# A fused two-block transformer kernel: row sums of the local softmax moved behind the next slot's transposes, and a scheduling fence behind the gated product

## The chip, the cores and the metric

The kernel runs on one core of a Trainium2 chip, as one launch. A core has a matrix engine (PE), a vector engine (DVE), an activation engine (ACT), a general engine (POOL) and a queue engine (SP) that issues the transfers. Each works through its own list of instructions in the order in which they were written down at build time; between engines only semaphores order the work. The metric is the device time of the launch in microseconds (us): the median of three runs of the kernel before is 5724.81 us (5724.38 to 5730.4).

## What is computed

The input is `x`, 8 batches of 512 tokens of width 128, in float32. The first part adds a causal attention with 16 heads of width 8, whose weights come from four Newton steps and not from a softmax. The change does not touch it. The second part is a small transformer of 6 layers on the layer-normed result; in each layer, for each batch:

```
q, k, v = split(shift(x) @ Wqkv)                # 16 heads of width 64
q, k    = rotary(l2norm(q) * qs), rotary(l2norm(k) * ks)
attn    = softmax(8 * q @ k.T, over a window of 32 back)
x       = x + (attn @ v) @ Wo
a, gate = split(layernorm(shift(x)) @ W1 + b1)  # 341 columns each
x       = x + (a * gelu(gate)) @ W2 + b2
```

`shift` moves half of the channels by one token. A softmax row is exp(s - max) divided by its own sum: that sum and the division are the steps that the change moves. The "first factor" of the feed-forward is `a`, and its products with W1 are those called `ap` in the code.

## The kernel before

The second part treats a layer, a batch and half of the heads (8 of 16) as a *half*, and each half as four *pairs* of heads. One turn of the loop in lines 713 to 753 is a *slot*; eight slots are one batch of one layer, so there are 48 batches to go through. In slot t four pieces of work overlap:

- the pair of slot t is begun. `turn` (L528) transposes its queries and keys on PE into `ptq` and copies them by ACT into `qT` (L540). `weigh` (L543) multiplies them into the scores `s` (L559), lets DVE find the row maxima and subtract them (L565, L566, into the tile `pr`), ACT take the exponential (L570), DVE sum each row (L572, `rs`) and invert the sum (L573), and POOL multiply the row by it (L574);
- the pair of slot t-2 (`LAG` is 2) is ended. `turn_weights` (L578) transposes `pr` on PE into `pT` (L584) and copies it by ACT into `prT` (L585); `gather` (L587) multiplies by the values into `po` (L594), copied by ACT (L601); `leave` (L603) adds the output product into `acc` (L607);
- a quarter of the half after the next is prepared. `prepare_qk` multiplies for the queries and keys (`m`, L476); ACT squares (L481), DVE sums (L482) and applies the rotary tables (L484, L492), POOL adds and normalizes (L496, L504), with an inverse root in between (L499 on DVE, L500 and L501 on ACT). `prepare_v` makes the values (`pv`, L512) and ACT copies them (L516) into `v`; after the fourth quarter `spread` (L518) copies `v` by four transfers on SP into the layout `v3`. There is one `v` tile, so the next copy into it waits for these transfers;
- one step of the feed-forward of the batch before: a generator (L622) that is advanced once per slot at L741. Its steps are the shifted input, the mean, the variance, the products `gp` of the gate (L645) with DVE adding the bias (L648), the products `ap` of the first factor (L655) with DVE multiplying them into the gate (L658), and the last product `y` (L665). The gelu of the gate (L618) is put by `gelus` (L613) between two fences of one slot, because it needs another activation table.

Below, the slot whose feed-forward step makes `ap` is called the *ap slot*, and the next one the *y slot*. In program order the DVE multiplications L658 come at the end of the ap slot.

PSUM tiles with the tag "mm" (`ptq`, `pT`, `m`, `pv`, `gp`, `ap`, `y` and others) share four buffers, which go round. A product can be started only when the engine that reads the old contents of its buffer is done. `pr` has three buffers, `rs` two.

The order of the instructions on each engine isn't the order of the program text. A list scheduler goes over all instructions at build time, with its own estimates of when inputs are ready, and takes among ready ones the earliest in the text. A fence (`tc.no_sync_barrier()`) is a rule for that scheduler alone: on each engine, what stands in the text before the fence is put before what stands after it. It adds no instruction and no semaphore.

Of the kernel before, what the change touches and what calls it, by code (L numbers as in the profile page):

```python
# [49 lines left out]
def tile_kernel(  # L50
# [402 lines left out]
    def shifted(b, name):  # L453

        xs = tp.tile([P, N], F32, name=name)
        hf = D // 2
        nc.gpsimd.tensor_copy(xs[0:hf, :], xT[0:hf, b, :])
        nc.gpsimd.memset(xs[hf:D, 0:1], 0.0)
        nc.gpsimd.tensor_copy(xs[hf:D, 1:N], xT[hf:D, b, 0 : N - 1])
        return xs  # L460
# [67 lines left out]
    def turn(a):  # L528

        g, p = a["g"], a["p"]  # L530
        a["qT"] = qT = []
        for t in range(2):
            pt = ps_a.tile([P, N], F32, name="ptq", tag="mm")
            for c in range(NT):
                nc.tensor.transpose(  # L535
                    pt[:, c * P : (c + 1) * P],
                    g["qn"][t][:, c, 2 * p : 2 * p + 2, :].rearrange("p h e -> p (h e)"), ident,
                )
            q = tp.tile([P, N], F32, name=f"qT{t}")
            nc.scalar.copy(q, pt)  # L540
            qT.append(q)

    def weigh(a):  # L543

        qT = a["qT"]
        a["pr"] = pr = tp.tile([P, 2, NT, KB], F32, name="pr", bufs=3)
        nm = tp.tile([P, 2, NT], F32, name="nm")
        s = [ps_b.tile([P, NT, KB], F32, name="s2") for e in range(2)]
        for e in range(2):
            nc.tensor.matmul(  # L550
                s[e].rearrange("p c k -> p (c k)"), lhsT=ident_h,
                rhs=band.rearrange("p c k -> p (c k)"), start=True, stop=False,
            )
        for n in range(NQ):
            c, u = n // 2, n % 2
            k0 = max(n * QB - WIN, 0)
            for e in range(2):
                hr = slice(e * DHL, (e + 1) * DHL)
                nc.tensor.matmul(  # L559
                    s[e][u * QB : (u + 1) * QB, c, KB - (n + 1) * QB + k0 : KB],  # L560
                    lhsT=qT[0][hr, n * QB : (n + 1) * QB], rhs=qT[1][hr, k0 : (n + 1) * QB],
                    start=False, stop=(n >= NQ - 2),
                )
        for e in range(2):
            nc.vector.tensor_reduce(nm[:, e], s[e], axis=AX.X, op=ALU.max, negate=True)  # L565
            nc.vector.tensor_tensor(  # L566
                pr[:, e], s[e], nm[:, e].unsqueeze(2).to_broadcast([P, NT, KB]), ALU.add
            )
        flat = pr.rearrange("p e c k -> p (e c) k")
        nc.scalar.activation(flat, flat, AF.Exp)  # L570
        rs = tp.tile([P, 2 * NT], F32, name="rs")
        nc.vector.tensor_reduce(rs, flat, axis=AX.X, op=ALU.add)  # L572
        nc.vector.reciprocal(rs, rs)  # L573
        nc.gpsimd.tensor_tensor(  # L574
            flat, flat, rs.unsqueeze(2).to_broadcast([P, 2 * NT, KB]), ALU.mult
        )

    def turn_weights(a):  # L578
        pr = a["pr"]
        a["prT"] = prT = tp.tile([KB, 2, NT, P], F32, name="prT")  # L580
        for e in range(2):
            pT = ps_a.tile([KB, NT, P], F32, name="pT2", tag="mm")
            for c in range(NT):
                nc.tensor.transpose(pT[:, c, :], pr[:, e, c, :], ident)  # L584
            nc.scalar.copy(prT[:, e], pT)  # L585
# [36 lines left out]
    def feed_forward(b, l, w1, w2):  # L622

        xs = shifted(b, "xf")
        yield
        mean = ps_a.tile([P, N], F32, name="mean", tag="mm")
        nc.tensor.matmul(mean, lhsT=ones_d, rhs=xs, start=True, stop=True)
        nc.vector.tensor_tensor(xs, xs, mean, ALU.subtract)
        sq = tp.tile([P, N], F32, name="sq")
        nc.scalar.activation(sq, xs, AF.Square)  # L630
        yield
        var = ps_a.tile([P, N], F32, name="var", tag="mm")
        nc.tensor.matmul(var, lhsT=ones_d, rhs=sq, start=True, stop=True)
        rn = tp.tile([P, N], F32, name="qr")
        nc.scalar.activation(rn, var, AF.Ln, bias=eps_ln)
        nc.scalar.activation(rn, rn, AF.Exp, scale=-0.5)
        nc.gpsimd.tensor_tensor(xs, xs, rn, ALU.mult)
        xn = tp.tile([P, N], F32, name="xn_ffn", bufs=1)
        nc.gpsimd.tensor_scalar(
            xn, xs, vec[:, 0, l : l + 1], vec[:, 1, l : l + 1], ALU.mult, ALU.add  # L640
        )
        yield
        for k, (c0, cn) in enumerate(CH):
            gp = ps_a.tile([P, N], F32, name="gp", tag="mm")
            nc.tensor.matmul(  # L645
                gp[:cn], lhsT=w1[:, DI + c0 : DI + c0 + cn], rhs=xn, start=True, stop=True
            )
            nc.vector.tensor_scalar(  # L648
                gate[:cn, k], gp[:cn], vec[:cn, 3 + NCH + k, l : l + 1], None, ALU.add
            )  # L650
        waiting.append(gate)
        yield
        for k, (c0, cn) in enumerate(CH):
            ap = ps_a.tile([P, N], F32, name="ap", tag="mm")
            nc.tensor.matmul(  # L655
                ap[:cn], lhsT=w1[:, c0 : c0 + cn], rhs=xn, start=True, stop=True
            )
            nc.vector.scalar_tensor_tensor(  # L658
                gate[:cn, k], ap[:cn], vec[:cn, 3 + k, l : l + 1], gate[:cn, k],
                ALU.add, ALU.mult,  # L660
            )
        yield
        y = ps_a.tile([P, N], F32, name="y2", tag="mm")
        for k, (c0, cn) in enumerate(CH):
            nc.tensor.matmul(  # L665
                y, lhsT=w2[:cn, k, :], rhs=gate[:cn, k], start=(k == 0), stop=(k == NCH - 1)
            )
        nc.vector.scalar_tensor_tensor(
            xT[:, b, :], y, vec[:, 2, l : l + 1], xT[:, b, :], ALU.add, ALU.add
        )  # L670
        if l == DEPTH - 1:
            yield
            pf = ps_a.tile([P, NT, D], F32, name="pf", tag="mm")
            for c in range(NT):
                nc.tensor.transpose(pf[:, c, :], xT[:, b, c * P : (c + 1) * P], ident)
            nc.vector.tensor_tensor(x2[:, b], x2[:, b], pf, ALU.add)
            nc.sync.dma_start(out[b].rearrange("(c p) d -> p c d", p=P), x2[:, b])
# [13 lines left out]
    def open_half(i):  # L691
        l, b, hv = halves[i]
        groups.append(begin(l, b, hv, shifted(b, "xs") if hv == 0 else groups[-1]["xs"]))
# [17 lines left out]
    pairs, parts, acc = [], [], None  # L711
    t = -1
    while t < len(halves) * PH + LAG or parts:
        i, p = t // PH, t % PH
        a = done = ahead = None
        if 0 <= i < len(halves):
            a = dict(g=groups[i], p=p)
            pairs.append(a)
        if LAG <= t < len(pairs) + LAG:
            done = pairs[t - LAG]  # L720
        if a:
            turn(a)
        if done:
            turn_weights(done)

        i, c = (t + 1) // PH + 1, (t + 1) % PH
        if i < len(halves):
            if c == 0:
                open_half(i)
            ahead = groups[i]  # L730
            prepare_qk(ahead, wq[ahead["hv"]], tab[ahead["l"]], c)
        gelus()
        if a:
            weigh(a)
        if done:
            gather(done)
        if ahead:
            prepare_v(ahead, wq[ahead["hv"]], c)
            if c == PH - 1:
                prepared(ahead)  # L740
        parts = [n for n in parts if next(n, n) is not n]  # L741
        if done:
            l, b, hv = (done["g"][n] for n in ("l", "b", "hv"))
            if done["p"] == 0 and hv == 0:
                acc = ps_c.tile([P, N], F32, name="acc")
            leave(done, wo[hv], acc)
            if done["p"] == PH - 1:
                if b == NB - 1 and l + 1 < DEPTH:
                    wo[hv] = load_wo(l + 1, hv)
                if hv == 1:  # L750
                    nc.vector.tensor_tensor(xT[:, b, :], xT[:, b, :], acc, ALU.add)
                    parts.append(feed_forward(b, l, *w12[l]))
        t += 1
# [51 lines left out]
```

## Time and profile before

| quantity | value |
|---|---|
| median of three runs | 5724.81 us |
| the profiled execution, its own time | 5724.38 us |
| its span, first to last instruction | 5722.4 us |
| PE busy | 4686.3 us (82% of the span) |
| DVE busy | 4775.5 us (83%) |
| ACT busy | 4038.0 us (71%) |
| POOL busy | 3250.3 us (57%) |
| PE busy from 2600 to 3100 us | 484.67 of 500 us |
| DVE busy in the same stretch | 409.62 of 500 us |

The first part lasts until about 2100 us, and there DVE and ACT are the busiest. In the second part PE is busy nearly always, with its clock granted in full. The page's shares are means over both parts; a timeline lists the instructions of one engine in the order of time, with the idle time before each in brackets, and what ended it.

### The profile page before, as it was taken

What the parts mean: (1) busy time and instruction counts of PE and PEld (TensorE: products, weight loads), DVE (VectorE), ACT (ScalarE), POOL (GpSimd) and SP (SyncE); (2) the same over time, 40 slices, a digit from 0 to 9 for tenths busy, and PEclk for the clock granted to TensorE, in tenths of its full rate; (3) what the DMA queues carried; (4) which work ended last, traced back from release to release, by engine and by line L of the source; (5) the groups of instructions that cost most, each with busy time, mean ns of one, the idle gap of its engine ahead of it and who ended that gap; (6) DMA issues with size and microseconds to landing.
All of it is one profiled execution on the core that took longest, in us unless ns stands there. A gap on an engine that the chain in (4) does not pass through costs nothing.

```text
span 5722.4 us, 108133 instructions
## 1 busy us (share of the span) xinstructions
PE 4686.3 (82%) x40909; PEld 2744.5 (48%) x40909; DVE 4775.5 (83%) x12028; ACT 4038.0 (71%) x6458; POOL 3250.3 (57%) x2915
## 2 busy tenths in 40 slices
PE   4556566655666549999999999999999999999998
PEld 2223333332333225556656555555555655556665
DVE  8889898998989858888888888888888888888886
ACT  5788888888888856666666666666666666666665
POOL 1333233333323347777777677777777777777774
PEclk6555555555555569999999999999999999999999
DMA  0000000000000011111111211122111111121111
GB/s 17 1 0 1 1 1 1 1 1 0 1 1 1 1 39 44 44 47 47 46 44 42 58 47 40 39 51 53 44 44 44 52 44 42 47 58 45 47 42 34
DMA packets 106558, 173.16 MB, mean 30 GB/s; under 512 B 12816, under 2 KB 30008, under 8 KB 106040
## 3 DMA queue, kind: packets, MB, share of 16 engines
q1 hardware_dynamic: 106040, 166.25, 11.7%
q8 instruction: 325, 5.32, 0.4%
q14 instruction: 193, 1.58, 0.1%
HBM read 19.42 MB, written 2.10 MB: 4 GB/s over the span
## 4 chain that ended last, share of the span: by engine, by line
PE 39%; DVE 33%; ACT 20%; POOL 5%; issue 2%; DMA 0%; SPq 0%; POOLq 0%; ACTq 0%; DVEq 0%
DVE stw L244 9%; PE m L476 8%; PE po L594 4%; PE pT L584 4%; PE pv L512 4%; PE s L559 3%; ACT d L241 3%; ACT d L242 3%; DVE qr L492 3%; ACT qT L540 3%; DVE ss L482 3%; PE acc L607 3%; DVE rs L572 3%; DVE qn L484 3%; DVE ns L209 2%
## 5 line engine op out<-in xcount | busy, mean ns | idle before, releaser
L496 POOL TENSOR_TENSOR qn<-qn,qr 128x512 f32<-128x512 f32 x768 | 975.5, 1271 | 580.4 <-DVE qr L492 430.0
L244 DVE BATCH_NORM_STATS2 stw<-d 128x6 f32<-128x512 f32 (+3 forms) x2048 | 868.1, 476 | 76.7 <-ACT d L242 74.8
L504 POOL TENSOR_TENSOR qn<-qn,ss 128x512 f32<-128x512 f32 x768 | 784.6, 1042 | 40.5 <-ACT ss L501 36.8
L482 DVE TENSOR_REDUCE ss<-sq 128x8 f32<-128x512 f32 x768 | 522.2, 680 | 328.5 <-ACT sq L481 326.0
L574 POOL TENSOR_TENSOR pr<-pr,rs 128x768 f32<-128x768 f32 x384 | 564.0, 1469 | 382.9 <-DVE rs L573 249.1
L476 PE MATMUL m<-wqkv,xs 128*128 128x512 f32 x1536 | 738.4, 603 | 48.2 <-ACT qT L540 37.6
L222 POOL TENSOR_TENSOR d<-ns,dl 128x512 f32<-128x512 f32 (+1 forms) x192 | 288.1, 1500 | 641.6 <-DVE stw L244 388.8
L242 ACT ACTIVATE d<-d 128x1536 f32<-128x1536 f32 (+3 forms) x512 | 641.3, 1261 | 5.3
L204 PE MATMUL s<-kn,qj 32*128 32x512 f32 (+3 forms) x1024 | 420.0, 753 | 245.5 <-DVE mn L209 242.0
L572 DVE TENSOR_REDUCE rs<-pr 128x8 f32<-128x768 f32 x384 | 364.8, 950 | 287.7 <-ACT pr L570 287.5
L222 POOL TENSOR_TENSOR da<-ns,dl 128x2048 f32<-128x2048 f32 (+3 forms) x128 | 299.1, 2340 | 502.4 <-PE dTp L286 362.1
L492 DVE TENSOR_TENSOR qr<-m,tab 128x256 f32<-128x256 f32 x1536 | 571.2, 413 | 0.0
L286 PE MATMUL dTp<-ident,da 128*128 128x128 f32 x1280 | 382.4, 424 | 221.5 <-ACT da L270 107.4
L481 ACT ACTIVATE sq<-m 128x512 f32<-128x512 f32 x768 | 439.3, 601 | 129.3 <-PE m L476 83.1
L601 ACT COPY oT<-po 128x512 f32<-128x512 f32 x384 | 223.8, 583 | 413.5 <-PE po L594 407.9
L484 DVE TENSOR_TENSOR qn<-m,tab 128x512 f32<-128x512 f32 x768 | 514.7, 670 | 0.0
L540 ACT COPY qT<-ptq 128x512 f32<-128x512 f32 x768 | 416.5, 583 | 90.6 <-PE ptq L535 90.0
L585 ACT COPY prT<-pT 96x512 f32<-96x512 f32 x768 | 431.5, 584 | 62.6 <-PE pT L584 53.5
L293 PE MATMUL po<-dT,va 128*32 128x128 f32 x2560 | 333.5, 395 | 173.1 <-DVE dT L288 173.0
L535 PEld LDWEIGHTS ptq<-ident,qn 128*128 128x128 f32 x3072 | 358.8, 141 | 220.0 <-issue 111.5
L241 ACT ACTIVATE d<-ns,dl 128x512 f32<-128x512 f32 (+1 forms) x768 | 450.6, 654 | 14.2 <-DVE stw L244 14.2
L584 PE MATMUL pT<-ident,pr 128*96 128x128 f32 x3072 | 411.6, 274 | 55.8 <-DVE rs L573 46.2
(137 smaller groups left out, 9910.0 us busy)
## 6 DMA issues: line engine op xcount, KB each, us to landing
v<-v SPq DMA_DIRECT2D x192, 512.0 KB
v<-v SPq DMA_DIRECT2D x96, 256.0 KB
v<-v SPq DMA_DIRECT2D x96, 192.0 KB
wqkv<-in_L_ffn_Wqkv_dram SPq DMA_DIRECT2D x36, 256.0 KB
wo<-in_L_ffn_Wo_dram SPq DMA_DIRECT2D x12, 256.0 KB
x<-in_L_attn_x_dram SPq DMA_DIRECT2D x8, 256.0 KB
out_dram<-x SPq DMA_DIRECT2D x8, 256.0 KB
w<-in_L_ffn_W_dram SPq DMA_DIRECT2D x6, 341.0 KB
```

The costliest lines, as they stand in the source:

```text
L222: nc.gpsimd.tensor_tensor(d, ns, dl[:, 4 * j : 4 * j + 4].unsqueeze(2).to_broadcast(list(d.shape)), ALU.add)
L241: nc.scalar.activation(d[:, g, :], ns[:, g, :], AF.Ln, bias=dl[:, i : i + 1])
L242: nc.scalar.activation(d, d, AF.Exp, scale=-1.0)
L244: nc.vector.bn_stats(st[:, 4 * j + g].rearrange("p u k -> p (u k)"), d[:, g, :])
L476: nc.tensor.matmul(m.rearrange("p h e -> p (h e)"), lhsT=lhsT, rhs=wqkv[:, t, :], start=True, stop=True,)
L482: nc.vector.tensor_reduce(ss[:, t, :], sq, axis=AX.X, op=ALU.add)
L484: nc.vector.tensor_tensor(qc, m, tab[:, 2 * t, c, :].unsqueeze(1).to_broadcast([P, HH, DHL]), ALU.mult)
L492: nc.vector.tensor_tensor(qr[:, :, u, :], mh[:, :, 1 - u, :], sw.unsqueeze(1).to_broadcast([P, HH, hd]), ALU.mult,)
L496: nc.gpsimd.tensor_tensor(qc, qc, qr.rearrange("p h u e -> p h (u e)"), ALU.add)
L504: nc.gpsimd.tensor_tensor(qc, qc, ss[:, t, :].unsqueeze(2).to_broadcast([P, HH, DHL]), ALU.mult)
L540: nc.scalar.copy(q, pt)
L584: nc.tensor.transpose(pT[:, c, :], pr[:, e, c, :], ident)
```

## The change

The row sums, the inversion and the multiplication leave `weigh` and become a function `share`, which the loop calls one slot later: after that slot's `turn`, before `turn_weights` of the pair that ends. And `feed_forward` gets a fence behind the loop over `ap` and L658. Nothing else is changed; the same instructions work on the same tiles.

```diff
         flat = pr.rearrange("p e c k -> p (e c) k")
         nc.scalar.activation(flat, flat, AF.Exp)
+
+    def share(a):
+
+        flat = a["pr"].rearrange("p e c k -> p (e c) k")
         rs = tp.tile([P, 2 * NT], F32, name="rs")
         nc.vector.tensor_reduce(rs, flat, axis=AX.X, op=ALU.add)
         nc.vector.reciprocal(rs, rs)
...
                 ALU.add, ALU.mult,
             )
+        tc.no_sync_barrier()
         yield
         y = ps_a.tile([P, N], F32, name="y2", tag="mm")
...
         if a:
             turn(a)
+        if 1 <= t < len(pairs) + 1:
+            share(pairs[t - 1])
         if done:
             turn_weights(done)
```

## The prediction

> **What bounds the kernel now.** First the page's busy times, then the windows by stage: in the second part PE is busy 484.67 of 500 us, so only its waits can be won. Second, the waits of PE between 2600 and 5600 us, longest first (engine, line, what it waited for: us in total, times, longest):
>
> ```profile
> PE pT L584 <- DVE rs L573: 40.1, 40, 1.3
> PE m L476 <- ACT qT L540: 30.5, 35, 0.9
> PE s L550 <- DVE pr L566: 8.7, 36, 0.5
> PE ptq L535 <- DVE gate L658: 5.5, 4, 1.4
> ```
>
> Forty batches lie in that stretch, and the first wait comes once in each, about 1.0 us. Third, the timeline of PE around one of them, ordinary batch of layer 1; the last three lines are the following slot, which isn't disturbed:
>
> ```profile
> 3314.17 1.04 PE L535 MATMUL ptq<-ident,qn 128*128 128x128 f32 x8
> 3316.17 1.27 PE L584 MATMUL pT<-ident,pr 128*96 128x128 f32 x8 [0.97 <-DVE rs L573]
> 3317.28 1.88 PE L476 MATMUL m<-wqkv,xs 128*128 128x512 f32 x4
> ...
> 3325.73 1.04 PE L535 MATMUL ptq<-ident,qn 128*128 128x128 f32 x8
> 3326.60 1.04 PE L584 MATMUL pT<-ident,pr 128*96 128x128 f32 x8
> 3327.47 1.88 PE L476 MATMUL m<-wqkv,xs 128*128 128x512 f32 x4
> ```
>
> From the first `ptq` to the first `m` it takes 3317.28 - 3314.17 = 3.11 us in the y slot and 3327.47 - 3325.73 = 1.74 us in the next: 1.37 us lost, of which the wait shows 0.97; the rest is stretch (`pT` 1.27 for 1.04) and the gap around the wait. Fourth, DVE, ACT and POOL at the same time:
>
> ```profile
> 3312.00 1.01 DVE L566 TENSOR_TENSOR pr<-s,nm 128x384 f32<-128x384 f32 x2
> 3312.93 0.74 DVE L658 SCALAR_TENSOR_TENSOR gate<-ap,vec,gate 128x512 f32<-128x512 f32 x1
> 3314.42 0.95 DVE L572 TENSOR_REDUCE rs<-pr 128x8 f32<-128x768 f32 x1 [0.75 <-ACT pr L570]
> 3315.29 0.74 DVE L658 SCALAR_TENSOR_TENSOR gate<-ap,vec,gate 128x512 f32<-128x512 f32 x1
> 3315.95 0.19 DVE L573 RECIPROCAL rs<-rs 128x8 f32<-128x8 f32 x1
> 3316.05 0.69 DVE L658 SCALAR_TENSOR_TENSOR gate<-ap,vec,gate 85x512 f32<-85x512 f32 x1
> 3318.97 0.69 DVE L482 TENSOR_REDUCE ss<-sq 128x8 f32<-128x512 f32 x1 [2.23 <-ACT sq L481]
> ```
>
> ```profile
> 3313.53 0.86 ACT L570 ACTIVATE pr<-pr 128x768 f32<-128x768 f32 x1
> ...
> 3323.35 0.58 ACT L516 COPY v<-pv 128x512 f32<-128x512 f32 x1
> ```
>
> ```profile
> 3314.54 2.04 POOL L504 TENSOR_TENSOR qn<-qn,ss 128x512 f32<-128x512 f32 x2
> 3316.55 1.47 POOL L574 TENSOR_TENSOR pr<-pr,rs 128x768 f32<-128x768 f32 x1
> ```
>
> The row sum sits between the first and the second L658 and waits 0.75 us for the exponential, which ACT ends at 3314.39. In the built program the first `pT` goes into the buffer that the second L658 reads and the second `pT` into that of the third. So PE waits for L658 at 3316.03; the profile names L573 because it ran alongside. What PE needs is stuck behind a sum that nobody needs yet.
>
> **What the skill says.** "TensorE: Matmul & The Clock Gate", section "Architectural detail", has ACT and DVE as strict FIFO; the trace agrees, L658 stood 0.75 us behind a row sum. "SBUF — State Buffer", section "Who interferes with whom", says that a `tensor_scalar` in a 2-port mode and a POOL instruction shut each other out for a whole instruction. The trace fits at 3341.04: L499 took 1.59 us instead of 0.16, up to the end of a POOL L496 (3341.34 to 3342.60), and the second row of waits is its sequel. "TensorE: Matmul & The Clock Gate", section "What's actually happening", has PE's clock halved after idleness: in two batches the `m` after this wait took 3.07 us instead of 1.88.
>
> **The change, part by part.** No instruction is added or removed, no transfer is added or moved on SP's queue. On DVE, in 46 of 48 batches, three L658 now stand together ahead of L572 and L573, and in the gate slot (`gp`) the third L648 stands ahead of L572. On ACT one `v` copy L516 in the y slot moves ahead of L500 and L501. On POOL the two L504 of the ap slot move ahead of the two copies of the shifted input, their clears too. PE's order is the same; one `m` in the gate slot waits for L648 instead of an ACT copy.
>
> *The three L658.* They start at 3312.93, 3313.59 and 3314.25 (0.66 apart, as their starts go back to back) and end at 3314.95. The first `pT` may start one step after `ptq`, at 3314.17 + 0.87 = 3315.04, and the second buffer it needs is free at 3314.33, the third at 3314.95. Both ahead of PE, so no wait. `m` then starts at 3315.91; it needs the `qT` copies, which ACT ends at 3315.87 as before. Gain 3317.28 - 3315.91 = 1.37 us.
>
> *The row sum, later.* L572 goes from 3314.42 to 3314.87, L573 ends at about 3316.0 instead of 3316.14. Its reader, L574 on POOL, is behind L504 and the copies until about 3316.4 either way, and its product is needed by a `pT` eleven us later. Cover on DVE: the 2.23 us of idleness before 3318.97, which become about 1.6 (next L482 at 3318.97 - 1.37 = 3317.60). Cost nothing; without it, at most the 0.45 us by which L572 slips.
>
> *POOL.* L504 twice (2.04), clears (0.2) and copies (1.2) in another order, same sum, ending at about 3316.4 as before. The shifted input is for a batch prepared five slots later. Cost nothing.
>
> *The gate slot.* L572 is 0.66 us later there, L573 0.1 us; L574 starts at 3306.65 in the trace and its `pT` is more than nine us away. The third L648 ends near 3305.2, the `m` that waits for it starts at about 3306.4 (second of the pair of 3305.59). Nothing.
>
> *The `v` copy and its transfers.* It waits in ACT's queue for the last transfer out of `v`; behind it stand L500, L501 and the exponential. Those transfers are issued on SP at 3313.66 to 3316.92, at the same times after the change, and move data until about 3320.6; the last landing recorded is 3321.45. The copy could start when `pv` is done, 3321.32 + 1.13 - 1.37 = 3321.1, so it waits until about 3321.5 and ends at 3322.1. L500 would be due at 3322.95 - 1.37 = 3321.6, so L500 and L501 slip by 0.5 us, to 3322.6. L504 follows on POOL at 3322.8, after L496. Covered by 0.2 us; if that is gone, L504 slips, and no `ptq` needs its product for several slots. PE pays only if the landing is over 1.6 us later than now.
>
> *Batches with new tables.* In five of the 46, `tables` (2.50 us on DVE) delays L658. There `ptq` to `pT` is 3.92 us instead of 2.01, and to `m` 5.03 (three) or about 5.4 (two, which lose 1.2 to 1.3 more at half clock). The second `ptq` waits for the first L658 before and after, 1.97 us after the first one; then the second and third L658 end at 3165.03 and 3165.69, `pT` starts 2.6 us after `ptq`, its second half after 3.3, `m` after 3.73. Gain 1.30 for three, and 1.7 to 2.9 for two, according to whether the clock still falls; I take 2.3.
>
> *Sum.* 41 x 1.37 + 3 x 1.30 + 2 x 2.3 = 56.2 + 3.9 + 4.6 = 64.7 us. Everything after the y slot waits for PE or follows it, so the gain should be carried on. Span 5722.4 - 64.7 = 5657.7; the profiled execution's own time 5724.38 - 64.7 = 5659.7, and the median, 0.4 us above it, 5660.
>
> **Rivals.** *Only the visible wait goes.* If `m` meets another limit (the `qT` copies leave 0.04 us), the gain is 46 x 0.97 = 45 us: 5680. Against it: the undisturbed slot has the same distance from `ptq` to its copies and no gap.
>
> *The other wait goes too.* The clash of L499 with POOL hangs on less than half a us: in layer 6 the clearing of `v3` comes 0.48 us before L499 instead of 0.18, the 0.87 us wait is missing and the batch takes 73.15 instead of 74.10 us. If the change shifts POOL by that much, 35 to 38 batches gain 0.95 more: 5625. Against it: two slots lie between, with POOL waiting for PE in both, so they are shifted as one.
>
> *No difference.* That holds if PE did wait for L573's result, through POOL, and not for L658. The `pr` that this `pT` reads was multiplied a slot earlier, ending at 3308.1, which speaks against it: 5725.
>
> *Slower: two new clashes.* POOL's and ACT's new order could bring L499 in the ap and the y slot under a POOL instruction. One such clash costs PE 0.87 us now; two cost 1.74, so 46 x (1.74 - 1.37) = 17 us more: 5742. It decides from the second clash per batch on; one alone leaves 46 x 0.5 = 23 us of gain. Against it: L499 of the ap slot (3310.99) comes before anything that moved, and that of the y slot has POOL waiting for the same DVE row.
>
> **How the numbers follow.** Chances: forecast 0.75, visible wait only 0.07, other wait too 0.07, one clash 0.03, no difference 0.03, slower 0.05. Differences under 0.2% (11 us) are about what a measurement of this kernel can't tell from none. Faster 0.92, same 0.03, slower 0.05. The forecast's own range is 5654 to 5668 (the clock, 46 or 45 batches, the slip of ACT). Taking in the visible wait alone and part of the other gives 5638 to 5682 for 8 in 10.
>
> **What would show it.** In the changed profile, the three L658 back to back, then L572 without the idleness of 0.75 us; no `pT` wait of 40 us in PE's list; `ptq` to `m` 1.74 us in the y slot; 72.7 us per ordinary batch. The `m` wait for `qT` stays near 30 us and `v` L516 shows a short idle time for a transfer. It is wrong if `pT` still waits, if L499 shows 1.6 us in more slots, or if another row of PE's waits grows by 40 us.

## The result, and the profile after

The median after the change is 5670.2 us over four runs (5667.55 to 5672.61), against 5724.6 us before (four runs, 5724.23 to 5730.4): a ratio of 0.9903, with a 95% interval from 0.9885 to 0.992. The median lies inside the predicted range of 5638 to 5682 us, 10 us above the predicted 5660, and 2 us outside the narrower range of 5654 to 5668 that the forecast gave to its own mechanism. The profiled execution took 5667.55 us with a span of 5665.8 us, so its span is 56.6 us shorter than the one before; 64.7 us were predicted.

The page's first part gives busy time, share of the span and number of instructions for each engine. Every engine named in it has as many instructions as before (the total counts others too), and PE's busy time is only 15 us shorter: most of what went is waiting.

```profile
span 5665.8 us, 108225 instructions
...
PE 4671.7 (82%) x40909; PEld 2749.7 (49%) x40909; DVE 4786.1 (84%) x12028; ACT 4029.4 (71%) x6458; POOL 3254.1 (57%) x2915
```

The lines of the code have moved: L658 (products of the first factor into the gate) is now L662, L572 and L573 (row sum, inversion) L576 and L577, L574 (multiplication on POOL) L578, L584 (`pT`) L588. Up to L570 nothing has moved. The waits of PE between 2600 and 5550 us, longest first, as before (engine, line, what it waited for: us in total, times, longest):

```profile
PE m L476 <- ACT qT L540: 30.8, 35, 0.9
PE s L550 <- DVE pr L566: 9.9, 37, 0.5
PE ptq L535 <- DVE gate L662: 8.9, 4, 2.2
```

The row of `pT`, 40.1 us, is gone. The `m` row stands, as predicted. But the last row, four waits of batches with new tables, has grown from 5.5 to 8.9 us: that was not predicted, and the missing gain lies in these batches. First the ordinary batch. PE in the y slot of one of them, in order of time (start, duration, engine, line, operation):

```profile
3297.25 1.04 PE L535 MATMUL ptq<-ident,qn 128*128 128x128 f32 x8
3298.12 1.04 PE L588 MATMUL pT<-ident,pr 128*96 128x128 f32 x8
3299.00 1.88 PE L476 MATMUL m<-wqkv,xs 128*128 128x512 f32 x4
```

From `ptq` to `m` it takes 1.75 us instead of 3.11, with no idle time and `pT` at its undisturbed 1.04 us. DVE at the same time has the three L662 back to back in one row (x3), and the row sum after them without a wait:

```profile
3296.01 2.06 DVE L662 SCALAR_TENSOR_TENSOR gate<-ap,vec,gate 128x512 f32<-128x512 f32 x3
3297.99 0.94 DVE L576 TENSOR_REDUCE rs<-pr 128x8 f32<-128x768 f32 x1
3298.96 0.20 DVE L577 RECIPROCAL rs<-rs 128x8 f32<-128x8 f32 x1
3300.69 0.69 DVE L482 TENSOR_REDUCE ss<-sq 128x8 f32<-128x512 f32 x1 [1.52 <-ACT sq L481]
```

The 0.75 us for which the row sum had blocked DVE have become part of what follows: 1.52 us of idleness are left in front of L482, where there were 2.23.

The other side is a batch with new tables. In the ap slot of every eighth batch DVE also makes the rotary tables of the next layer (L439). Before the change, DVE and PE show there (start, duration, and in brackets the idle time ahead and what ended it):

```profile
3159.36 2.50 DVE L439 SCALAR_TENSOR_TENSOR tab<-rot_sb,qks 128x256 f32<-128x256 f32 x4
...
3162.46 0.60 PE L535 MATMUL ptq<-ident,qn 128*128 128x128 f32 x4
3164.43 0.66 PE L535 MATMUL ptq<-ident,qn 128*128 128x128 f32 x4 [1.37 <-DVE gate L658]
3166.39 1.72 PE L584 MATMUL pT<-ident,pr 128*96 128x128 f32 x8 [1.30 <-DVE rs L573]
3167.90 3.07 PE L476 MATMUL m<-wqkv,xs 128*128 128x512 f32 x4
```

And after it, in the same batch:

```profile
3144.18 3.34 DVE L439 SCALAR_TENSOR_TENSOR tab<-rot_sb,qks 128x256 f32<-128x256 f32 x4
...
3146.14 2.28 POOL L504 TENSOR_TENSOR qn<-qn,ss 128x512 f32<-128x512 f32 x2
...
3147.27 0.60 PE L535 MATMUL ptq<-ident,qn 128*128 128x128 f32 x4
3150.09 0.65 PE L535 MATMUL ptq<-ident,qn 128*128 128x128 f32 x4 [2.22 <-DVE gate L662]
3150.84 1.66 PE L588 MATMUL pT<-ident,pr 128*96 128x128 f32 x8
3152.29 3.10 PE L476 MATMUL m<-wqkv,xs 128*128 128x512 f32 x4
```

The four L439 take 3.34 us instead of 2.50. The second of them takes about 1.49 us in both kernels, beside a POOL L496. What is new is the fourth. Alone, before and after the change, it is:

```profile
3161.45 0.41 DVE L439 SCALAR_TENSOR_TENSOR tab<-rot_sb,qks 128x256 f32<-128x256 f32 x1
```

```profile
3146.26 1.26 DVE L439 SCALAR_TENSOR_TENSOR tab<-rot_sb,qks 128x256 f32<-128x256 f32 x1
```

After the change it starts 0.12 us behind POOL's L504 (3146.14), which the change moved forward; before, POOL was clearing and copying there. Both work on operands in SBUF. The first L662 comes 0.85 us later, and PE's wait in the middle of `ptq` grows from 1.37 to 2.22 us. The wait for `pT` is gone here too, but of the 1.30 us that it gave only some 0.4 are left.

The `m` behind these waits runs at half clock in this batch both before and after (3.07 and 3.10 us for 1.88), so the batch still gains 0.38 us, from 77.61 to 77.23. In three of the other four the clock had stayed full before and falls after the change, and they lose 0.95 to 1.3 us each. In the last it is the other way round: 77.70 us before, 75.61 after.

Counted from the last product of one `ap` to that of the next, the 48 batches give a balance of the 56.6 us. Ordinary batches take 74.10 us before and 72.73 to 72.77 after:

| part | before | after | change of the span |
|---|---|---|---|
| ordinary batch, up to and in layer 5 (35) and last layer (5) | 74.10 and 73.15 us | 72.75 and 71.79 us | 40 x -1.352 = -54.1 us |
| the rest, to the end | | | -2.5 us |
| five batches with new tables, mean | 76.67 us | 76.84 us | +0.9 us |
| of the 40, batches longer than the others by 0.28 us | two | six | +1.1 us |
| up to the first `ap` | 2269.9 us | 2268.0 us | -1.9 us |

The last row is nearly all the first part of the kernel, in which nothing is changed: the first `ptq` comes 2.2 us earlier than before. In the profiles shown here its time to the first `ap` is anywhere between 2263.8 and 2280.6 us, so comparisons of profiles are made below by the periods of the batches, which repeat to a few hundredths of a us.

### The profile page after: what moved, and what is told of

It reads as the page before. It is cut to its first block, busy times and chain, and to the rows that moved or that the text cites. A ratio compares the mean times of both kernels' runs of the same rounds, so it can differ in the third digit from the quotient of the medians.

```text
span 5665.8 us, 108225 instructions
## 1 busy us (share of the span) xinstructions
PE 4671.7 (82%) x40909; PEld 2749.7 (49%) x40909; DVE 4786.1 (84%) x12028; ACT 4029.4 (71%) x6458; POOL 3254.1 (57%) x2915
## 4 chain that ended last, share of the span: by engine, by line
PE 45%; DVE 33%; ACT 15%; POOL 5%; issue 2%; DMA 0%; SPq 0%; POOLq 0%; ACTq 0%; DVEq 0%
DVE stw L244 9%; PE m L476 8%; PE po L598 5%; PE pv L512 5%; PE pT L588 4%; PE s L559 4%; PE acc L611 3%; ACT d L241 3%; ACT d L242 3%; DVE qr L492 3%; ACT qT L540 3%; DVE ss L482 3%; PE ptq L535 3%; DVE qn L484 3%; DVE ns L209 2%
## 5 line engine op out<-in xcount | busy, mean ns | idle before, releaser
L496 POOL TENSOR_TENSOR qn<-qn,qr 128x512 f32<-128x512 f32 x768 | 976.9, 1272 | 508.3 <-DVE qr L492 359.0
L504 POOL TENSOR_TENSOR qn<-qn,ss 128x512 f32<-128x512 f32 x768 | 786.4, 1045 | 50.9 <-ACT ss L501 50.2
L578 POOL TENSOR_TENSOR pr<-pr,rs 128x768 f32<-128x768 f32 x384 | 564.8, 1471 | 386.3 <-DVE rs L577 178.0
L476 PE MATMUL m<-wqkv,xs 128*128 128x512 f32 x1536 | 740.1, 605 | 48.0 <-ACT qT L540 37.9
L482 DVE TENSOR_REDUCE ss<-sq 128x8 f32<-128x512 f32 x768 | 522.5, 680 | 289.8 <-ACT sq L481 287.0
L204 PE MATMUL s<-kn,qj 32*128 32x384 f32 (+3 forms) x1024 | 419.4, 751 | 245.8 <-DVE mn L209 242.6
L576 DVE TENSOR_REDUCE rs<-pr 128x8 f32<-128x768 f32 x384 | 364.2, 948 | 258.0 <-ACT pr L570 258.0
L540 ACT COPY qT<-ptq 128x512 f32<-128x512 f32 x768 | 417.0, 583 | 86.1 <-PE ptq L535 85.4
L286 PEld LDWEIGHTS dTp<-ident,da 128*128 128x128 f32 x1280 | 213.5, 203 | 479.7 <-issue 204.1
L598 PE MATMUL po<-prT,v 96*64 96x64 f32 x12288 | 443.6, 225 | 0.5 <-ACT prT L589 0.4
```

Source lines behind the costliest of these rows:

```text
L286: nc.tensor.transpose(pt[:, kb, :], d[:, g, kb * P : (kb + 1) * P], ident)
L476: nc.tensor.matmul(m.rearrange("p h e -> p (h e)"), lhsT=lhsT, rhs=wqkv[:, t, :], start=True, stop=True,)
L482: nc.vector.tensor_reduce(ss[:, t, :], sq, axis=AX.X, op=ALU.add)
L496: nc.gpsimd.tensor_tensor(qc, qc, qr.rearrange("p h u e -> p h (u e)"), ALU.add)
L504: nc.gpsimd.tensor_tensor(qc, qc, ss[:, t, :].unsqueeze(2).to_broadcast([P, HH, DHL]), ALU.mult)
L598: nc.tensor.matmul(po[e * DHL : (e + 1) * DHL, n * QB : (n + 1) * QB], lhsT=g["v3"][:, n, h * DHL : (h + 1) * DHL], rhs=prT[:, e, n // 2, ...
```

## The experiments

The theory is that of the prediction: in the y slot PE waits for the second and third L658, which are stuck behind the row sum; moving the sum behind them frees PE. Its rivals: PE waits for the row sum itself or what hangs on it; and one of the two parts of the change does all of it. A second question came with the result: is it really L504 beside L439 that ate the gain of the batches with new tables (the table batches below)? A third is the wait that stayed, `m` for `qT`, and whether it is a clash of L499 with POOL as the prediction read it.

### Each part alone

The first kernel keeps the move of the sums and leaves the fence out:

```diff
                 ALU.add, ALU.mult,
             )
-        tc.no_sync_barrier()
         yield
```

> The share function alone, without the fence. In the built program the gate slot has the order of the changed kernel, but in the ap slot the row sum still stands between the first and the second product of the gate; only the inversion goes behind the third. POOL and ACT stand as before. If PE waits for the second product (my theory), the wait of pT stays at about 1.0 us in each batch, and the time is 5716 to 5725 us. If PE waited for the inverted sums, which come 0.6 us later here, it would be 46 x 0.6 = 28 us slower than before, 5750. If the calling place alone did the work, 5670.

It took 5721.8 us (12 runs; before, 5726.46), a ratio to before of 0.9992, with a 95% interval of [0.9983, 1.0]: hardly anything. An ordinary batch takes 74.03 us instead of 74.10. DVE in the y slot, and PE beside it:

```profile
3306.18 0.74 DVE L662 SCALAR_TENSOR_TENSOR gate<-ap,vec,gate 128x512 f32<-128x512 f32 x1
3307.66 0.95 DVE L576 TENSOR_REDUCE rs<-pr 128x8 f32<-128x768 f32 x1 [0.74 <-ACT pr L570]
3308.53 1.40 DVE L662 SCALAR_TENSOR_TENSOR gate<-ap,vec,gate 128x512 f32<-128x512 f32 x2
3309.85 0.19 DVE L577 RECIPROCAL rs<-rs 128x8 f32<-128x8 f32 x1
```

```profile
3309.42 1.21 PE L588 MATMUL pT<-ident,pr 128*96 128x128 f32 x8 [0.97 <-DVE gate L662]
```

The sum stands later in the text, and the scheduler still puts it between the first and the second L662, where it waits 0.74 us for the exponential as before. One thing has changed: the inversion now comes after all three L662. So it no longer runs alongside the second, and the list of waits has a new name in the same wait of the same length:

```profile
PE pT L588 <- DVE gate L662: 40.1, 40, 1.3
```

Before, that row named the inversion, `rs` L573. Here `pT` starts at 3309.42, ahead of the inversion at 3309.85, and the wait is as long as it was: PE doesn't wait for the inversion, nor for anything behind it. It waits for L662, and "no difference", the rival that depended on L573, falls with it.

The second kernel keeps the fence and puts the sums back where they were:

```diff
         nc.scalar.activation(flat, flat, AF.Exp)
-
-    def share(a):
-
-        flat = a["pr"].rearrange("p e c k -> p (e c) k")
         rs = tp.tile([P, 2 * NT], F32, name="rs")
...
-        if 1 <= t < len(pairs) + 1:
-            share(pairs[t - 1])
```

> The fence alone, with the row sums in their old place. DVE's order is exactly that of before; on POOL the two L504 of the ap slot and on ACT the v copy of the y slot move ahead. My theory: the pT wait stays, ordinary batches take 74.1 us. In the five batches with new tables, the tables on DVE (two inputs in SBUF) run against L504 on POOL and take 3.3 us instead of 2.5, as in the changed kernel, so 5 x 0.85 = 4 us and up to 5 x 1.3 us of halved clock more: 5725 to 5736. Rival, that the moves on POOL and ACT bring the gain: 5670.

It took 5736.03 us (20 runs), a ratio of 1.0019 [1.0012, 1.0026]: slightly slower, at the upper end of what was expected. An ordinary batch takes 74.10 us, as before the change, and PE's waits are those of before but for the last row:

```profile
PE pT L584 <- DVE rs L573: 39.1, 39, 1.3
PE m L476 <- ACT qT L540: 31.4, 36, 0.9
...
PE ptq L535 <- DVE gate L658: 8.9, 4, 2.2
```

DVE's order is the old one here, since the sum comes ahead of the fence in the text. What the fence does move is POOL's L504, ahead of the copies of the shifted input, and that alone brings the longer tables: a table batch takes 78.36 us, against a mean of 76.67 before. Some 0.85 us of that are the tables; the rest is the clock, for `m` begins at half clock in all five of them here and in two before. The six batches that are longer by 0.28 us (74.38) come with the fence too; the sum-only kernel has two, as the kernel before. So the gain is an interaction: the sum must come later in the text, and the fence must hold the scheduler to it. The loss comes with the fence: the sum-only kernel's table batches take 75.95 us (one, at half clock, 77.64), as before the change or a little less.

### The tables taken off DVE

If L504 beside L439 is what keeps the table batches from gaining, they should gain in full once the tables aren't made on DVE. That is necessary and not sufficient, since the edit takes the tables off DVE's queue whatever made them longer. The third kernel is the changed one with the tables on POOL; the constant factor is multiplied into the scales once, in the first layer. The fourth is the kernel before with the same edit.

```diff
         for k in range(4):
-            nc.vector.scalar_tensor_tensor(
-                tab[:, k], rot_sb[:, k], root * QK_SCALE if k < 2 else root,
-                qks[:, k, l, :].unsqueeze(1).to_broadcast([P, NT, DHL]), ALU.mult, ALU.mult,
+            if l == 0:
+                nc.vector.tensor_scalar(
+                    qks[:, k], qks[:, k], root * QK_SCALE if k < 2 else root, None, ALU.mult
+                )
+            nc.gpsimd.tensor_tensor(
+                tab[:, k], rot_sb[:, k],
+                qks[:, k, l, :].unsqueeze(1).to_broadcast([P, NT, DHL]), ALU.mult,
             )
```

> The changed kernel with the tables of the next layer made by POOL in four products instead of by DVE (the scalar is multiplied into the small scale tile once at the start). If the five table batches are slow because the tables stand in front of the gate's products on DVE, they should fall from 76.84 us on average to the ordinary 72.74: 5 x 4.1 = 20 us less than the changed kernel, 5650, up to 5655 if POOL is late with something. If the weight loads of the next layer or something else there costs the time, it stays at 5670.

> The kernel before with the tables made by POOL. Its five table batches should fall from 76.67 us on average to 74.1, 13 us in all: 5712. The difference to the changed kernel with the same edit should be 46 x 1.37 = 63 us: with the tables out of the way the change is worth in every batch what it is in an ordinary one. If the change had a second cost in the table batches, the difference stays at 55.

The third took 5651.82 us (four runs, ratio to before 0.9869 [0.9852, 0.9885]), and each of its table batches 72.73 us, as an ordinary one. The fourth took 5712.38 us (11 runs, 0.9977 [0.9968, 0.9986]), and its table batches 74.10 us. Without tables on DVE the change is worth 60.6 us, and from the first `ap` to the last one 61.3 us. In the list of waits of the third kernel only the two rows are left that have to do with neither the sums nor the tables (L480 and L544 are L476 and L540, L554 and L570 are L550 and L566):

```profile
PE m L480 <- ACT qT L544: 31.4, 36, 0.9
PE s L554 <- DVE pr L570: 9.8, 37, 0.5
```

One row for each kernel with the table instructions alone (number, then shortest, median and longest in ns) shows where the time came from. Before, and after the change:

```profile
L439 DVE SCALAR_TENSOR_TENSOR tab<-rot_sb,qks x20: 409/414/1490, 2564.7 to 4949.1; 128x256 f32<-128x256 f32 x20
```

```profile
L439 DVE SCALAR_TENSOR_TENSOR tab<-rot_sb,qks x20: 411/838/1491, 2557.6 to 4904.9; 128x256 f32<-128x256 f32 x20
```

With the fence alone, without the moved sums:

```profile
L439 DVE SCALAR_TENSOR_TENSOR tab<-rot_sb,qks x20: 409/837/1492, 2568.3 to 4959.7; 128x256 f32<-128x256 f32 x20
```

With both parts and the tables on POOL:

```profile
L443 POOL TENSOR_TENSOR tab<-rot_sb,qks x20: 717/720/726, 2571.9 to 4902.5; 128x256 f32<-128x256 f32 x20
```

The medians mislead here, because there are groups with nothing between them. Before, 15 of the 20 take 0.41 us, and five, the second in each batch, 1.49 us beside POOL's L496. In the changed kernel and in the fence-only one the fourth in each batch takes 1.26 us too; each time L504 has started 0.11 to 0.12 us earlier. The sum-only kernel, in which L504 stays where it was, has none of these. That ties the longer tables to L504. On POOL the twenty take 717 to 726 ns each, without a long one.

### The wait that stayed

The prediction put the second row, `m` for `qT`, down to a clash: the clearing of the first rows of `v3` on POOL (L521) comes shortly before L499, POOL's L496 then starts ahead of L499, and L499 takes 1.59 us instead of 0.16. If so, the wait must go with the clearing. In the fifth kernel two fixed `v3` tiles have their first rows cleared once, at the start, and no longer for each half.

```diff
+    v3s = [vp.tile([KB, NQ, HC], F32, name=f"v3{u}", bufs=1) for u in range(2)]
+    for u in range(2):
+        nc.gpsimd.memset(v3s[u][0:WIN, 0, :], 0.0)
...
-        v3 = vp.tile([KB, NQ, HC], F32, name="v3")
+        v3 = v3s[len(groups) % 2]
...
-        nc.gpsimd.memset(v3[0:WIN, 0, :], 0.0)
```

> The changed kernel with the zero rows of the two v3 buffers cleared once at the start instead of by a POOL clear in every half (94 clears fewer; nothing else writes there). If the remaining wait of PE, m for qT, comes from L499 on DVE being shut out by a POOL L496 that the clear has made late, it goes: 35 of the batches fall from 72.74 to about 71.8 us, 35 x 0.95 = 33 us less than the changed kernel, 5637. If that wait has another cause, it stays near 30 us in PE's list and the time at 5670.

It took 5610.06 us (four runs; before, in the same session, 5725.57 us; ratio 0.98 [0.9786, 0.9815]), where 5637 was expected. The mechanism holds: the row of `m` is gone, and with it most of the row of `s`:

```profile
PE ptq L538 <- DVE gate L665: 8.9, 4, 2.2
PE s L553 <- DVE pr L569: 1.7, 5, 0.4
```

L499 itself shows it as well. From 2600 to 5550 us, in the changed kernel and in this one (there it is L503), again with the shortest, median and longest in ns:

```profile
L499 DVE TENSOR_SCALAR ss<-ss x323: 159/163/1612, 2607.4 to 5547.4; 128x16 f32<-128x16 f32 x162
L503 DVE TENSOR_SCALAR ss<-ss x329: 164/167/171, 2601.3 to 5546.2; 128x16 f32<-128x16 f32 x165
```

In the changed kernel 35 of them take over 1 us, as many as there are waits in the row; here none does.

The expected gain was too small. An ordinary batch went from 72.75 to 71.37 us, 1.38 us and not 0.95: the slot of the clash gave 1.13 us (8.74 to 7.61), and the two after it 0.08 and 0.15 us, where the `s` of the mean slot waits. In the last layer, where the wait was missing before, the batch stays at 71.8 us. The table batches gained 9.7 us together, of which 5 x 1.375 is the same thing; most of the rest is the clock, which now falls in two of them and not in four. 35 x 1.375 and 9.7 make up the 57.8 us between the first `ap` and the last full batch.

The sixth kernel has both edits, the tables on POOL and the clearing done once.

> Both edits on the changed kernel: tables on POOL and the zero rows cleared once. If the two costs are independent they add: 5651.8 - 33 = 5619 us, every batch at about 71.8 us. If POOL's tables fill the room that the clears left, the table batches stay some tenths longer.

It took 5599.04 us (four runs, 5588.09 to 5612.05; ratio 0.9785 [0.9766, 0.9804]), the lowest median of all kernels here, where 5619 was expected. Two of its runs, though, lie within the range of the fifth kernel (5608.27 to 5620.67 us), and the other two at 5588 and 5590. By the periods the order is clear: ordinary and table batches alike take 71.37 us, and from the first `ap` to the last it is 18.7 us shorter than the fifth kernel and 55.2 us shorter than the third. So the two edits add, to within 2 us, and what was too low in the expectation is the gain of the clearing. The view by stretches for 3000 to 3500 us, in the order PE, PEld, DVE, ACT, POOL, granted clock, DMA share, GB/s:

```profile
3000.00:3500.00 500.00, 497.88 (x5197) 310.15 (x5196) 421.74 (x904) 342.47 (x660) 370.44 (x341) 1.00 0.20 49
```

PE is busy 497.88 of 500 us there, and was busy 482.48 in the kernel before. In this stage hardly any wait on another engine is left to be won: 1.7 us in all from 2600 to 5500 us.

## Why the prediction was right, and where it missed

**What bounds the kernel: right.** The `pT` row of 40.1 us was a real wait on the path, and the profile's name for it, L573, was the wrong one. The sum-only kernel shows this: it moves L573 out of the way, and the wait keeps its place and length under the name L662.

**The three L658: right to a few hundredths.** Predicted were starts 0.66 us apart, `ptq` to `m` in 1.74 us, 1.37 us per batch and 72.7 us per period. Measured: 2.06 us for the three, 1.75 us, 1.35 us, 72.75 us. The order that the built program showed on DVE is what made this easy to forecast. Neither the move of the sums alone nor the fence alone gave that order.

**The row sum, later: right.** L572 was to slip by 0.45 us and then cost nothing; against the `ptq` beside it, it starts 0.74 us after (3297.99 against 3297.25), and 0.70 was predicted. DVE's idleness in front of L482 is 1.52 us for the predicted 1.6.

**The `v` copy and its transfers: the direction right, the size off.** The copy was to wait some 0.4 us for the last transfer out of `v`, and L500 and L501 to slip by 0.5. ACT in the y slot after the change:

```profile
3305.16 0.59 ACT L516 COPY v<-pv 128x512 f32<-128x512 f32 x1 [1.42 <-DMA v<-v]
3305.65 0.22 ACT L500 ACTIVATE ss<-ss 128x16 f32<-128x16 f32 x1
3305.90 0.22 ACT L501 ACTIVATE ss<-ss 128x16 f32<-128x16 f32 x1
```

ACT is idle for 1.42 us. The `pv` products end at 3304.16, so the copy is 1.0 us late; L500 comes at 3305.65, where 3304.66 would have been its time without the new order (3322.95 before, less 1.37 and less the 16.92 us between the two places). It slips by 1.0 us, twice the forecast. The cover of 0.2 us on POOL is used up: L504 waits 0.36 us for L501. But the second cover held. The y slot is shorter by 1.37 us in full (11.56 to 10.19), and the exponential starts where it would have. Of the 1.6 us that the prediction left for a later landing before PE would pay, some 0.6 are used (the copy at 3305.16 where 3321.5 - 16.92 = 3304.6 was forecast).

**POOL, "same sum, cost nothing": this step failed**, and with it the term for the batches with new tables. The sum of POOL's work is the same, and in ordinary batches the order does cost nothing. In the five others it puts L504 beside the tables. The prediction took 2.50 us for them from the trace of before and did not ask what POOL would do beside them at the new place. The Trainium skill states a reason in the very section that the prediction cited ("SBUF — State Buffer", "Who interferes with whom"): a DVE instruction with two inputs in SBUF contends with a POOL instruction that reads SBUF. L439 has two such inputs and L504 reads SBUF; the trace agrees, with 0.84 us for four. The section was used for L499 and not for L439, at the next place where something moved. In place of a gain of 3.9 + 4.6 = 8.5 us the five batches lost 0.9. The forecast that the second `ptq` waits 1.97 us after the first one, as before, is the sentence that is wrong: it waits 2.82 us.

**The clock in those batches.** Two of five ran into half clock before, and four of five after; the forecast had at most two. That is about half of what is missing in these batches. At full clock such a batch went from 76.01 to 75.61 us: it gained 0.4 us and not 1.30, so the tables took 0.9 us from each of the five, 4.5 us in all. The other 4.9 us are the clock: the forecast counted on 2 us from it, and instead two more batches than before ran into half clock, which costs a batch 1.4 to 1.7 us. "TensorE: Matmul & The Clock Gate", section "What's actually happening", gives an idle window of about 3.4 us for the fall. Here it falls after a single idle stretch of 2.22 us, with some work on either side. It doesn't fall each time: after the same stretch it stayed full in one of five batches of the changed kernel and in three of five of the fifth one. How the granted clock follows from such shorter gaps isn't settled by these runs.

**The sum.** Of the 8.1 us between the predicted and the measured change of the span, 9.4 are the table batches and 1.1 the batches that are longer by 0.28 us. The ordinary batches and the rest to the end gave 0.4 us more than 41 x 1.37, and 1.9 us came from before the first `ap`, where no gain was forecast: that is chance. With the fence the 0.28 us fall on one batch in each layer, eight batches apart. Why isn't known.

**The rivals.** "Only the visible wait" falls: `ptq` to `m` reached 1.75 us, so the stretch went too. "The other wait goes too" didn't happen, as the row of 30.8 us shows, but its mechanism is real, as the fifth kernel shows, and worth 1.38 us a batch where it was priced at 0.95. "Two new clashes" was the right kind of danger: one new clash did come, with L439 and not with L499, in five batches and not in 46.

## What to carry to other kernels

A wait is named after the instruction that ended last beside it; ask which buffer the waiting instruction needs, and who reads its old contents, before you decide what to move. When an edit moves work on POOL, list what DVE does at the new place and see which of it has two inputs in SBUF or is a small `tensor_scalar`: the cost appears in DVE's durations, not in POOL's sum. A place in the text and a fence are two halves of one change where a list scheduler decides: either half alone brought next to nothing here, and the fence alone a small loss, because it also reorders the engines that it was not meant for.

## What was not expected of the hardware

Beside POOL's L504 the fourth L439 went from 0.41 to 1.26 us, and the two L504 together only from 2.04 to 2.28 us. The L439 had started 0.12 us after the first L504: the one that came second paid most of it. And two clearings a batch on POOL, of 0.52 us each, cost the kernel 1.38 us in each batch up to layer 5, because one of them brought a `tensor_scalar` of 128x16 elements, 0.16 us by itself, under the POOL instruction that followed it: it then took 1.59 us.
